# Transposes as two 64-row halves beside half-array matmuls in a PixArt block

## The chip, the core and the metric

The kernel runs on one core of a Trainium2 chip. The metric is the device time of one execution in microseconds (us); three runs of the kernel before have a median of 804.1 us. TensorE (PE) multiplies matrices into PSUM, VectorE (DVE) and ScalarE (ACT) work on PSUM and SBUF, GpSimd (POOL) on SBUF alone, and SyncE (SP) issues nearly all DMAs.

## The reference

A diffusion-transformer block for a batch of 16 sequences of 256 tokens with 256 features, all in float32: self-attention with 16 heads of 16, cross-attention to 256 context tokens, and an MLP of width 1024.

```python
x_norm = modulate(_ln(x), shift_a, scale_a)
q, k, v = split(x_norm @ W_qkv + b_qkv)              # 16 heads of 16
attn = softmax(q @ k.T * scale) @ v
x = x + gate_a[:, None] * (attn @ W_proj + b_proj)
q_c = _ln(x) @ W_qc + b_qc
k_c, v_c = split(_ln(context) @ W_kvc + b_kvc)
x = x + (softmax(q_c @ k_c.T * scale) @ v_c) @ W_cproj + b_cproj
x_norm2 = modulate(_ln(x), shift_m, scale_m)
x = x + gate_m[:, None] * (gelu(x_norm2 @ W_mlp1 + b_mlp1) @ W_mlp2 + b_mlp2)
```

## The kernel before, in words

The two attentions of a sequence are two *units*, a self unit (`s`) and a cross unit (`c`); 32 units run in a fixed order that soon alternates between the kinds. The MLP follows the last unit. A unit's stages are spread over several turns of the loop, so that each turn of `beat(n, k)`, k = 0 to 7, holds work of five or six units. All engines run in the order in which the program is written.

Float32 precision comes from pairs: a matrix is cut into a high part in the format fp32r (`xTh`, `h_q`) and the rest (`xTl`, `l_q`), and three products are added. A *lane* (`lane`) is a projection, Q, K, V or the output projection P, over one half of the contraction, 64 rows: 12 matmuls that use the upper or the lower half of the PE array. `lanes(x, y)` runs half 0 of one projection beside half 1 of another, matmul by matmul; both halves of a projection add into one PSUM tile, in two different beats. Names of lanes in the profile: `ps_q`, `ps_k`, `ps_v_s`, `ps_P_s` of self units, `ps_qc`, `ps_kc`, `ps_v_c`, `ps_P_c` of cross units.

Every beat begins with a *visit* (`visit`): four matmuls `s` of the next unit's scores, by which VectorE finds the maxima (`mx`, `s_tile`), and four matmuls `st` of this unit's transposed scores (`t_part`), which ScalarE exponentiates into `pt` (`exp`, gathered by `exps()`). `s` and `st` have two PSUM banks each and a single buffer; only in beat 6 of some units (`light`) half of `s` goes to another bank. Beats 0 and 4 hold the products with V (`av_part`, tile `o`, 16 matmul calls that the profile shows as 32), and beats 1, 3, 5 and 7 hold lanes.

Transposes with the full array come in between, through two shared PSUM buffers (tag `tr`, also used for `o`):

- `m_part` transposes the maxima (`psm`), ScalarE negates them, and SP sends them by DMA into row 63 of the queries: second half of unit n in beat 0, first half of unit n+1 in beat 4;
- `p1.turn(hf)` transposes the attention output (`psA`, four 128x128 pieces) in beats 2 and 6; VectorE divides by the sums (`norm`, tiles `rc` and `A`);
- `transposed(...)` makes the pair `xTh`, `xTl` of a normalized input (`psT_s`, `psT_c`, `psT_q`) or of `A` (`psT_as`, `psT_ac`), in beats 2, 4 and 6. `high` is ScalarE's. `low` is VectorE's for self units; elsewhere (`low_pool`) ScalarE makes a float32 copy `y` and GpSimd subtracts.

In PSUM, the tiles of lanes take turns in two buffers with the tag `gen`. The last three units (`whole`) project with the full array (`psP_c`), since the lanes run out.

Of the kernel before, what the change touches and what calls it, by code (L numbers as in the profile page):

```python
# [21 lines left out]
def pixart_block(  # L22
# [63 lines left out]
    vts = [const.tile([P, NT, NH, 32], F32, name=f"v{i}") for i in range(3)]  # L86
    wself = const.tile([P, 16, H], F32R, name="wself")
# [218 lines left out]

    def transposed(src, name, scale=None, pool=False):

        o = Box()

        def turn():
            o.ps = ps_gen(f"psT_{name}", SHORT)
            for f in range(KC):
                for t in range(NT):
                    PE.transpose(o.ps[:, f * N + t * P:f * N + (t + 1) * P],
                                 src()[:, t, f * P:(f + 1) * P], ident)
# [33 lines left out]
        o.turn, o.high, o.low = turn, high, low_pool if pool else low  # L350
        return o

# [17 lines left out]
    def lane(o, half):  # L370


        rows = slice(half * 64, half * 64 + 64)
        for low in (False, True):
            for f in range(2):
                for k in range(KC):
                    for a, b in (((1, 0),) if low else ((0, 0), (0, 1))):
                        xT, W = o.src.xT, o.W
                        x_, w_ = xT[a][rows, k], W[b][rows, k]
                        if o.tok:  # L380
                            x_ = x_[:, f * P:(f + 1) * P]
                        else:
                            w_ = w_[:, f * P:(f + 1) * P]
                        PE.matmul(o.ps[:, f * N:(f + 1) * N], *((x_, w_) if o.tok else (w_, x_)),
                                  start=o.fresh, stop=(half == 1 and low and k == KC - 1),
                                  skip_group_check=True)
                        o.fresh = False
                        yield

    def lanes(x, y):  # L390


        if x:
            x.ps, x.fresh = ps_gen(f"ps_{x.name}", LONG), True
        return zip_longest(*(lane(o, half) for half, o in enumerate((x, y)) if o))

    def run(steps, n=12):
        for _ in islice(steps, n):
            pass
# [92 lines left out]
    def build_pre(u):  # L492

        b = u.b
        u.mx = None
# [20 lines left out]
    def build_post(u):  # L516
# [17 lines left out]

        def turn(hf):
            o.ps = ps_gen(f"psA{hf}_{name}", SHORT)
            for t in range(NT):
                for r in range(2):
                    PE.transpose(o.ps[:, (2 * t + r) * P:(2 * t + r + 1) * P],
                                 u.oT[hf][:, r, t * P:(t + 1) * P], ident)  # L540
# [45 lines left out]
        u.post = o  # L586
# [8 lines left out]
    def s_tile(u, g, par, t, bank=None, home=sp):  # L595
# [14 lines left out]
        if u.mx is None:  # L610
            u.mx = work.tile([P, 2, 2, 4, NT], F32, tag="mx", name=f"mx_{u.n}", bufs=3)
        mx = u.mx.rearrange("p f r a t -> p r f a t")
        a = slice(2 * (g % 2), 2 * (g % 2) + 2)
        if alone or apart:
            src = home[bank] if apart else sp[:, bank]
            DVE.tensor_reduce(mx[:, par, g // 2, a, t], src.rearrange("p (j n) -> p j n", j=2),
                              AX.X, ALU.max)
        elif bank == 1:
            DVE.tensor_reduce(mx[:, :, g // 2, a, t], home.rearrange("p r (j n) -> p r j n", j=2),
                              AX.X, ALU.max)  # L620
        yield

    def m_part(u, hf):

        pst = ps_gen(f"psm_{u.n}_{hf}", SHORT)
        PE.transpose(pst[:16, :P], u.mx[:, hf].rearrange("p r a t -> p (r a t)"), ident)
        m = work.tile([16, P], F32R, tag="m", name=f"m_{u.n}_{hf}", bufs=1)
        ACT.mul(m, pst[:16, :P], -1.0)
        for par in range(2):
            SP.dma_start(u.q[par * 64 + 63:par * 64 + 64, 4 * hf:4 * hf + 4, :].bitcast(F32),  # L630
                         m[par * 8:(par + 1) * 8].bitcast(F32))
# [321 lines left out]

    def beat(n, k):
        if n < 0:
            visit(n, k, (st, sp)[k % 2])
            return
# [4 lines left out]
        whole = n > nu - 4  # L962
# [4 lines left out]
        q3T = q3  # L967
# [21 lines left out]
        visit(n, k, home)  # L989
        if k == 0:  # L990
            if cur:
                m_part(cur, 1)
            exps()
# [14 lines left out]
        elif k == 1:  # L1008
            exps()
            run(lanes(q2 and q2.Q, p2))  # L1010
# [3 lines left out]
        elif k == 2:  # L1014
            exps()
            if prev:
                p1.turn(1)
            if q3T:
                q3T.T[0].turn()
                q3T.T[0].high()  # L1020
            if prev:
                p1.norm(1)
            if p2 and p2.hurry:
                p2.add()
        elif k == 3:
            exps()
            if q3T and q3T.kind == "s":
                q3T.T[0].low()
            run(lanes(q2 and q2.V, q2 and q2.Q))
            if q3T and q3T.kind == "c":  # L1030
                q3T.T[0].low()
        elif k == 4:
            if nxt:
                m_part(nxt, 0)
            exps()
# [3 lines left out]
            if prev:  # L1039
                p1.aT.turn()  # L1040
                p1.aT.high()
# [11 lines left out]
        elif k == 5:  # L1053
            exps()
            run(lanes(q3 and q3.K, q2 and q2.V))
            if prev:
                p1.aT.low()
# [11 lines left out]
        elif k == 6:  # L1069
            exps()  # L1070
            if cur:
                cur.post.begin()
                cur.post.turn(0)
            if lx:
                lx.T[1].turn()
                lx.T[1].high()
# [3 lines left out]
            if prev and whole:  # L1080
                p1.proj(0)
                p1.proj(1)
        elif k == 7:
            exps()
            run(lanes(None if whole else p1, q3 and q3.K))
            if prev and whole:
# [5 lines left out]
            if lx:  # L1092
                lx.T[1].low()
# [97 lines left out]
```

## Time and profile before

| what | value |
|---|---|
| median of 3 runs | 804.1 us (802.99 to 809.25) |
| the profiled execution, first to last instruction | 801.2 us |
| busy time of PE, DVE, ACT, POOL | 780.7, 596.9, 583.5, 465.1 us |
| granted clock of TensorE, mean | 0.997 |
| GpSimd, subtraction of a low part, 128x512 | 1280 ns |
| ScalarE, high part, 128x512 | 588 ns |

The profiled execution is a run of its own; its span is 2.9 us under the median of the three, and no other time of it is given. Busy times overlap, and a busy PE need not be at its peak. In a profile row, "x4" is the count of instructions; `xTl_as<-y_as,xTh_as` reads output and inputs; what stands behind "idle" or in brackets names who ended the idle time ahead. A line number is that of a helper (L51) through which the kernel issues everything, so rows are told apart by the names of the tiles.

### The profile page before, as it was taken

To read this page: it belongs to the slowest core of one execution; us is meant where nothing else is said; L and a number is where in the kernel's file an instruction comes from. 1 tells how busy PE (TensorE), PEld (TensorE's weight loads), DVE (VectorE), ACT (ScalarE), POOL (GpSimd) and SP (SyncE) were. 2 spreads that over 40 slices of the span, in tenths; PEclk is the share of its full clock that TensorE was granted. 3 is DMA by queue.
4 is the path that set the end of the run, shared out by engine and by line. 5 is a ranking of instruction groups with operands and counts; after the bars stand their busy time and mean duration, and the time that the engine had idled before them with its cause. 6 is when DMAs were issued, how large, how long until landed. Compare 5 with 4: busy or idle time off the path is not lost.

```text
span 801.2 us, 23698 instructions
## 1 busy us (share of the span) xinstructions
PE 780.7 (97%) x9447; PEld 658.7 (82%) x9447; DVE 596.9 (74%) x1063; ACT 583.5 (73%) x1024; POOL 465.1 (58%) x405
## 2 busy tenths in 40 slices
PE   9999999999999999999999999999899999999997
PEld 8677777878878878877887787777669999999997
DVE  5887878788888878878888887876764656656662
ACT  4278888878888887878888788887656666666663
POOL 6745647565463756646475677563536656666653
PEclk9999999999999999999999999999999999999999
DMA  7554444434343453535445454534311322321211
GB/s 212 142 157 121 119 124 114 125 103 141 107 135 108 134 138 100 144 102 142 108 126 149 128 147 118 153 102 121 96 43 42 92 60 60 81 58 62 80 44 50
DMA packets 89938, 87.88 MB, mean 110 GB/s; under 512 B 9506, under 2 KB 85572, under 8 KB 89828
## 3 DMA queue, kind: packets, MB, share of 16 engines
q1 hardware_dynamic: 89364, 85.58, 38.4%
q8 instruction: 75, 1.23, 0.6%
q0 software_dynamic: 192, 0.52, 0.2%
q10 hardware_dynamic: 272, 0.26, 0.1%
q14 instruction: 35, 0.29, 0.1%
HBM read 26.97 MB, written 8.46 MB: 44 GB/s over the span
## 4 chain that ended last, share of the span: by engine, by line
PE 78%; DVE 11%; ACT 3%; DMA 3%; POOL 2%; issue 2%; ACTq 0%; SPq 0%; POOLq 0%; DVEq 0%
PE s L51 17%; PE o L51 14%; PE ph L51 11%; PE st L51 11%; DVE mx L51 8%; PE ps_qc L51 4%; PE ps_q L51 3%; PE ps_kc L51 3%; ACT pt L51 2%; PE ps_P_s L51 2%; PE ps_v_s L51 2%; PE ps_k L51 2%; PE psm L51 2%; PE ps_P_c L51 2%; PE ps_v_c L51 1%
## 5 line engine op out<-in xcount | busy, mean ns | idle before, releaser
L51 DVE TENSOR_REDUCE mx<-s 128x4 f32<-128x1024 f32 (+1 forms) x267 | 309.3, 1163 | 93.9 <-PE s L51 91.0
L51 ACT ACTIVATE pt<-st 128x1024 f32<-128x1024 f32 x252 | 256.7, 1019 | 39.9 <-PE st L51 34.3
L51 PE MATMUL s<-big 63*128 63x256 f32 (+1 forms) x1024 | 122.0, 309 | 6.6 <-DVE mx L51 3.7
L51 PE MATMUL o<-pt,v 128*32 128x256 f32 x2048 | 125.0, 385 | 0.0
L51 POOL TENSOR_TENSOR hl<-hf,hh 128x512 fp32r<-128x512 f32 x64 | 88.9, 1398 | 54.8 <-ACT hh L51 53.8
L51 PEld LDWEIGHTS s<-big 63*128 63x128 f32 (+1 forms) x1024 | 80.8, 185 | 41.9 <-DVE mx L51 18.8
L51 PE MATMUL st<-big 64*128 64x256 f32 (+1 forms) x1024 | 108.7, 283 | 4.9 <-ACT pt L51 4.0
L51 PEld LDWEIGHTS o<-pt,v 128*32 128x32 f32 x2048 | 60.3, 110 | 41.2 <-issue 0.8
L51 PEld LDWEIGHTS st<-big 64*128 64x128 f32 (+1 forms) x1024 | 82.2, 186 | 9.5 <-ACT pt L51 7.2
L51 ACT ACTIVATE hf<-ph,bT 128x256 f32<-128x256 f32 x120 | 50.3, 473 | 28.1 <-PE ph L51 28.1
L51 ACT COPY oT<-o 128x512 f32<-128x512 f32 x63 | 37.0, 587 | 43.8 <-PE o L51 43.8
L51 ACT ACTIVATE hh<-ph,bT 128x256 fp32r<-128x256 f32 x120 | 50.4, 472 | 23.7 <-PE st L51 11.9
L51 POOL TENSOR_TENSOR xTl_c<-y_c,xTh_c 128x512 fp32r<-128x512 f32 x16 | 20.5, 1281 | 61.7 <-PE s L51 52.5
L51 POOL TENSOR_TENSOR xTl_as<-y_as,xTh_as 128x512 fp32r<-128x512 f32 x16 | 20.5, 1280 | 55.5 <-ACT y_as L51 55.5
L51 PE MATMUL ph<-wqch,wself 128*128 128x256 f32 x256 | 51.8, 285 | 0.0
L51 PE MATMUL ph<-wkch,wself 128*128 128x256 f32 x256 | 51.8, 286 | 0.0
L51 POOL TENSOR_TENSOR xTl_ac<-y_ac,xTh_ac 128x512 fp32r<-128x512 f32 x16 | 20.5, 1284 | 52.4 <-ACT y_ac L51 48.4
L51 PE MATMUL s<-big,hh 128*128 128x256 f32 x256 | 47.4, 282 | 0.0
L51 PE MATMUL st<-big,hh 128*128 128x256 f32 x256 | 47.2, 281 | 0.0
L51 DVE TENSOR_SCALAR xn_m<-x,mv_m,rs_m 128x256 f32<-128x256 f32 x32 | 38.3, 1238 | 11.4 <-POOL rs_m L51 11.4
L51 PEld LDWEIGHTS ph<-wqch,wself 128*128 128x128 f32 x256 | 42.0, 191 | 0.4 <-issue 0.4
L51 PEld LDWEIGHTS ph<-wkch,wself 128*128 128x128 f32 x256 | 41.9, 191 | 0.4
(223 smaller groups left out, 2378.1 us busy)
## 6 DMA issues: line engine op xcount, KB each, us to landing
big<-h_kc SPq DMA_DIRECT2D x64, 128.0 KB
big<-h_qc SPq DMA_DIRECT2D x64, 128.0 KB
big<-h_k SPq DMA_DIRECT2D x62, 128.0 KB
big<-h_q SPq DMA_DIRECT2D x62, 128.0 KB
big<-l_k SPq DMA_DIRECT2D x32, 128.0 KB
big<-l_q SPq DMA_DIRECT2D x32, 128.0 KB
c<-in_ctx_dram SPq DMA_DIRECT2D x16, 256.0 KB
g<-gd SPq DMA_DIRECT2D x16, 256.0 KB
```

Source lines behind the costliest of these rows:

```text
L51: i = f(*a, **k)
```

## The change

Every transpose inside the units becomes two halves of 64 rows each, which are written to 64 columns each of the same PSUM bank, and each half runs beside lane matmuls in the other half of the array. Between the two halves stands an instruction of TensorE that waits for the last matmul of the half before (`after`); lanes get such a wait ahead of half 1 too. `transposed` gets an `evac` (ScalarE, float32 copy) and a `cut` (GpSimd: cast to the high part, then subtraction). The maxima lie in fixed tiles of 160 columns, so that their transpose has 128 columns of weights; GpSimd zeroes these tiles at the start.

```diff
+    def after(name):
+        gate = PE.nop()
+        tc.add_manual_dep(gate.ins, name, mybir.DependencyInfo(
+            mybir.DependencyClass.Sync, mybir.DependencyReason.DATA), reason="one bank, two halves of the array")
+
+    def half_turns(pieces, o):
+        done = []
+        def half(h):
+            rows = slice(64 * h, 64 * h + 64)
+            for i, p in enumerate(pieces):
+                if i == 0 and done:
+                    after(done[0])
+                ins = PE.transpose(o.ps[:, i * P + 64 * h:i * P + 64 * h + 64], p[rows], ident[rows, rows])
+                if i == len(pieces) - 1:
+                    done.append(ins.ins.name)
+                yield
+        return half(0), half(1)
...
+        def evac():
+            y = o.y = work.tile([P, KC, N], F32, tag="y", name=f"y_{name}", bufs=2)
+            if scale is None:
+                ACT.copy(y.rearrange("p k n -> p (k n)"), o.ps)
+            else:
+                for f in range(KC):
+                    ACT.activation(y[:, f], o.ps[:, f * N:(f + 1) * N], AF.Identity, scale=scale[f])
+
+        def cut():
...
+            POOL.tensor_copy(hi, o.y)
+            POOL.tensor_tensor(lo, o.y, hi, ALU.subtract)
...
+        if half:
+            after(o.seen)
...
+    def take(it, n):
+        for _ in range(n):
+            next(it, None)
+            yield
+
+    def beside(a, b):
+        for _ in zip_longest(chain(*a), chain(*b)):
             pass
...
         visit(n, k, home)
+        exps()
         if k == 0:
-            if cur:
-                m_part(cur, 1)
-            exps()
...
         elif k == 1:
-            exps()
-            run(lanes(q2 and q2.Q, p2))
+            m = m_halves(cur, 1) if cur else none
+            x, y = lane0(q2 and q2.Q), lane1(p2)
+            beside([m[0], x], [take(y, 4), m[1], y])
+            if cur:
+                m_send(cur, 1)
...
         elif k == 2:
-            exps()
-            if prev:
-                p1.turn(1)
-            if q3T:
-                q3T.T[0].turn()
-                q3T.T[0].high()
-            if prev:
-                p1.norm(1)
+            T = q3.T[0].halves() if q3 else none
+            A = p1.halves(1) if prev else none
+            x, y = lane0(q2 and q2.V), lane1(q2 and q2.Q)
+            beside([T[0], A[0], take(x, 2)], [take(y, 10)])
+            rest_x, rest_y = [x], [T[1], A[1], y]
...
         elif k == 3:
-            exps()
-            if q3T and q3T.kind == "s":
-                q3T.T[0].low()
-            run(lanes(q2 and q2.V, q2 and q2.Q))
-            if q3T and q3T.kind == "c":
-                q3T.T[0].low()
+            beside(rest_x, rest_y)
+            if q3:
+                q3.T[0].evac()
+                q3.T[0].cut()
+            if prev:
+                p1.norm(1)
         elif k == 4:
-            if nxt:
-                m_part(nxt, 0)
-            exps()
             if cur:
                 av_part(cur, 0)
                 av_part(cur, 1)
-            if prev:
-                p1.aT.turn()
-                p1.aT.high()
...
         elif k == 5:
-            exps()
-            run(lanes(q3 and q3.K, q2 and q2.V))
+            m = m_halves(nxt, 0) if nxt else none
+            aT = p1.aT.halves() if prev else none
+            x, y = lane0(q3 and q3.K), lane1(q2 and q2.V)
+            beside([m[0], take(x, 7), aT[0], x], [take(y, 2), aT[1], m[1], y])
+            if nxt:
+                m_send(nxt, 0)
             if prev:
-                p1.aT.low()
+                p1.aT.evac()
+                p1.aT.cut()
...
         elif k == 6:
-            exps()
             if cur:
                 cur.post.begin()
-                cur.post.turn(0)
-            if lx:
-                lx.T[1].turn()
-                lx.T[1].high()
+            T = lx.T[1].halves() if lx else none
+            A = cur.post.halves(0) if cur else none
+            y = lane1(q3 and q3.K)
+            beside([T[0], A[0]], [take(y, 8 if lx else 4)])
+            rest_y = [T[1], A[1], y]
...
         elif k == 7:
-            exps()
-            run(lanes(None if whole else p1, q3 and q3.K))
-            if prev and whole:
+            beside([lane0(None if apart else p1)], rest_y)
+            if lx:
+                lx.T[1].evac()
+                lx.T[1].cut()
+            if prev and apart:
```

`lane0` opens a projection's PSUM tile and yields half 0, `lane1` yields half 1, `m_halves` yields the two halves of the maxima's transpose, and `m_send` is the second part of the old `m_part`.

More of the change, by code (lines that the diff above doesn't have):

```diff
@@ L1 @@
 from collections import defaultdict
-from itertools import islice, zip_longest
+from itertools import chain, zip_longest
 from contextlib import ExitStack
@@ L86, in pixart_block @@
     vts = [const.tile([P, NT, NH, 32], F32, name=f"v{i}") for i in range(3)]
+    mxs = [const.tile([P, 160], F32, name=f"mx{i}") for i in range(3)]
+    for t_ in mxs:
+        POOL.memset(t_, 0.0)
     wself = const.tile([P, 16, H], F32R, name="wself")
@@ L350, in transposed @@
         o.turn, o.high, o.low = turn, high, low_pool if pool else low
+        o.halves, o.evac, o.cut = halves, evac, cut
         return o
@@ L533, in gate, with pieces, halves @@
             POOL.tensor_tensor(o.xg, X[b], bc_t(G[b][:, 1]), ALU.add)
+        def pieces(hf):
+            o.ps = ps_gen(f"psA{hf}_{name}", SHORT)
+            return [u.oT[hf][:, r, t * P:(t + 1) * P] for t in range(NT) for r in range(2)]
         def turn(hf):
[L536 to L540, printed above, removed]
+            whole(pieces(hf), o)
+        def halves(hf):
+            return half_turns(pieces(hf), o)
         def norm(hf):
```

71 lines of the change are left out of this document (42 added, 29 removed).

## The prediction

> **What bounds the kernel now.** I read the page's head and its chain of work first, then the busy time by stretches for two neighbouring units, then the timeline of one unit, engine by engine.
>
> ```profile
> span 801.2 us, 23698 instructions
> PE 780.7 (97%) x9447; PEld 658.7 (82%) x9447; DVE 596.9 (74%) x1063; ACT 583.5 (73%) x1024; POOL 465.1 (58%) x405
> PE 78%; DVE 11%; ACT 3%; DMA 3%; POOL 2%; issue 2%; ACTq 0%; SPq 0%; POOLq 0%; DVEq 0%
> ```
>
> ```profile
> 402.65:419.86 17.21, 17.00 (x246) 13.59 (x244) 15.58 (x30) 14.10 (x23) 11.90 (x11) 1.00 0.42 115
> 419.86:437.25 17.39, 17.29 (x251) 14.01 (x249) 13.43 (x22) 14.58 (x24) 7.56 (x8) 1.00 0.47 128
> ```
>
> Columns of the second fence: stretch, its length, then busy time of PE, PEld, DVE, ACT, POOL, granted clock, DMA share, GB/s. TensorE is busy all the time at full clock, and the chain is 78% TensorE. The first unit works on a cross-attention unit (call it C), the second on a self-attention unit (S); a pair takes 34.60 us. But VectorE has 15.58 of 17.21 us in C: there is little room below TensorE's time.
>
> One unit C on TensorE. Each `s` row that opens a visit starts a beat; the beats k=0 to 7 start at 402.65 (the stretch's start), 405.30, 407.29, 409.04, 411.03, 414.27, 416.26 and 417.45.
>
> ```profile
> 403.23 0.28 PE L51 MATMUL psm<-ident,mx 128*16 128x128 f32 x1
> 403.44 1.93 PE L51 MATMUL o<-pt,v 128*32 128x256 f32 x32
> 405.30 0.50 PE L51 MATMUL s<-big 63*128 63x256 f32 x4
> ...
> 407.29 0.42 PE L51 MATMUL s<-big 63*128 63x256 f32 x4
> 407.53 0.42 PE L51 MATMUL st<-big 64*128 64x256 f32 x4
> 407.88 0.66 PE L51 MATMUL psA_s<-ident,oT 128*128 128x128 f32 x4
> 408.38 0.60 PE L51 MATMUL psT_s<-ident,xn_s 128*128 128x128 f32 x4
> 409.04 0.50 PE L51 MATMUL s<-big 63*128 63x256 f32 x4
> ...
> 409.61 0.28 PE L51 MATMUL ps_v_c<-wvch,xTh_c 64*128 64x256 f32 x1
> ...
> 411.03 0.42 PE L51 MATMUL s<-big 63*128 63x256 f32 x4
> 411.62 0.28 PE L51 MATMUL psm<-ident,mx 128*16 128x128 f32 x1
> 411.82 1.93 PE L51 MATMUL o<-pt,v 128*32 128x256 f32 x32
> 413.69 0.66 PE L51 MATMUL psT_as<-ident,A_s 128*128 128x128 f32 x4
> 414.27 0.50 PE L51 MATMUL s<-big 63*128 63x256 f32 x4
> 416.26 0.43 PE L51 MATMUL s<-big 63*128 63x256 f32 x4
> 417.45 0.51 PE L51 MATMUL s<-big 63*128 63x256 f32 x4
> 418.11 0.50 PE L51 MATMUL st<-big 64*128 64x256 f32 x4
> ```
>
> Three prices come out of it. A slot (one half-array matmul in each half): 12 pairs from 409.61 to 411.03, so 0.118 us. A visit (`s` and `st`, four slots) is 0.47, and 0.57 right after full-array work (409.04 to 409.61), so 0.10 for the change of mode. A full transpose is 0.11: four of them take 0.60 (`psT_s`), one takes 0.28 (`psm`), and (0.60 - 0.28)/3 = 0.107.
>
> There is a second limit, the loop of the scores: `s` must wait until VectorE has reduced the last ones.
>
> ```profile
> 407.76 1.23 DVE L51 TENSOR_REDUCE mx<-s 128x4 f32<-128x1024 f32 x1
> 408.90 0.25 DVE L51 RECIPROCAL rc_s<-psA_s 128x16 f32<-128x16 f32 x1
> 409.18 0.42 DVE L51 TENSOR_TENSOR A_s<-psA_s,rc_s 128x256 f32<-128x256 f32 x1
> ```
>
> In k=2 `s` starts at 407.29, the reduce at 407.76, it ends at 408.99, and the next `s` is at 409.04: no ordinary beat can be shorter than 1.75 us, whatever TensorE saves in it.
>
> **The change, beat by beat.** TensorE first.
> - k=0 and k=4 lose `psm` (403.23 to 403.44 and 411.62 to 411.82: 0.2 each), k=4 also the four transposes of `A` (413.69 to 414.27: 0.58). Both become 2.44 to 2.46 (before 2.65 and 3.24).
> - k=1 has 13 slots instead of 12: 1.99 + 0.12 = 2.11. k=5 has 17: 1.99 + 5 x 0.118 = 2.58.
> - k=2 loses 8 full transposes (407.88 to 409.04, 1.16 with the drain) and gets 10 slots, 1.18; k=3 goes from 12 slots to 10 and has no mode to change. Both would be 0.47 + 1.18 = 1.65, so the score loop sets them: 1.75. k=2 gains nothing, k=3 0.24.
> - k=6 of S: 8 slots, 1.41, loop again, 1.75 as now. k=6 of C uses a second bank for `s` and goes below the loop; 4 slots, 0.94. k=7: 12 slots, 0.47 + 1.42 = 1.88, before about 2.0 in S.
>
> In C, k=7 now lasts 2.41 because `st` at 418.11 waits for ScalarE:
>
> ```profile
> 416.50 0.61 ACT L51 COPY v<-ps_v_c 128x512 f32<-128x512 f32 x1
> 417.03 1.02 ACT L51 ACTIVATE pt<-st 128x1024 f32<-128x1024 f32 x1
> ```
>
> That exponential stays behind `y` and `v`, which come later after a longer k=5: I place it 0.75 to 1.77 after k=6 starts, so `st` of k=7 at 1.84, and 0.24 + 1.42 of `st` pairs and slots behind it: k=6 and k=7 together 3.5, now 3.60.
>
> Then what VectorE, ScalarE and the waits give back. `norm(1)` (0.68, from 408.90 to 409.58) moves from k=2 to the end of k=3, ahead of the reduce of k=4. In S it pushes reduce, `l_q` and statistics so that the reduce of k=5 ends late: I estimate 0.03. In C, statistics and `rs_c` ahead of the reduce of k=2 make that beat an estimated 1.83. The scaled `y_s` of a self unit is two ScalarE passes like this one, behind the exponential of k=3:
>
> ```profile
> L51 ACT ACTIVATE xTh_s<-psT_s,sc 128x256 fp32r<-128x256 f32 x32 | 13.4, 472 | 6.6 <-PE psT_s L51 5.1 <-DVE sc L51 1.5
> ```
>
> They end about 2.6 after k=3 starts (the exponential from 0.75, its successor 0.9 later, then 2 x 0.47). `o` of k=4 takes the bank that they read and could start at 1.75 + 0.58 = 2.33, so it starts 0.25 late. VectorE is freed of `xTl_s`, two passes a pair. The self wait: for all but one of the ten or so waits in a unit, the last matmul of the first half lies at least six slots, 0.7 us, back, against 0.28 that a matmul takes: no stall. The transposes of `A` in k=5 alone have two slots between (0.24): one stall of 0.05 to 0.15, I take 0.1. A wait itself lies between 0 and the 0.10 of a mode change; I take 0, since five of them stand in beats that the score loop sets.
>
> C: 2.44 + 2.11 + 1.83 + 1.75 + 2.69 + 2.68 + 3.5 = 17.0. S: 2.44 + 2.11 + 1.75 + 1.75 + 2.44 + 2.68 + 1.75 + 1.88 + 0.03 = 16.8. The pair is 33.8 against 34.6: 0.8 gained. Bounds: with no give-back (0.08 + 0.25 + 0.03 and two stalls of 0.1) 1.4; with each wait outside the loop's beats (six a unit) at 0.05, 0.2.
>
> GpSimd makes both parts now. Its prices:
>
> ```profile
> L51 POOL TENSOR_TENSOR xTl_as<-y_as,xTh_as 128x512 fp32r<-128x512 f32 x16 | 20.5, 1280 | 55.5 <-ACT y_as L51 55.5
> L51 POOL CAST wkch<-wkc_f 128x512 fp32r<-128x512 f32 x1 | 0.6, 610 | 5.7 <-DMA wkc_f<-in_L_xcond_W_kvc_dram 5.7
> L51 POOL TENSOR_SCALAR xn_c<-c,mv_c,rs_c 128x256 f32<-128x256 f32 x32 | 38.9, 1224 | 1.7
> L51 POOL TENSOR_TENSOR rs_q<-rs_q,mhalf 128x2 f32<-128x2 f32 x16 | 11.4, 712 | 11.8 <-DVE rs_q L51 11.8
> L51 POOL TENSOR_TENSOR hl<-hf,hh 128x512 fp32r<-128x512 f32 x64 | 88.9, 1398 | 54.8 <-ACT hh L51 53.8
> ```
>
> Five casts (3.05) and one subtraction more (1.28): 19.5 + 4.3 = 23.8 of 33.8 us, not a bound by sum. The cover that matters is its queue in C. From `y_ac` in k=5 of S it does cast, subtraction, `rs_s`, `xn_s`, cast, subtraction, three adds of `x1` and its gate (1.28 each), `rs_c`, `xn_c`, and then the cast that k=5 of C needs in slot 2: 3 x 0.61 + 5 x 1.28 + 2 x 0.71 + 4 x 1.22 = 14.5, 14.9 with gaps. By my beats 14.9 is there. It costs nothing, with no reserve.
>
> The maxima go to the queue one beat later, and this moves SP's order:
>
> ```profile
> 411.75 2.48 SPq L51 DMA_DIRECT2D big<-h_qc  x4
> 414.33 1.42 SPq L51 DMA_DIRECT2D big<-m  x2
> 415.85 1.28 SPq L51 DMA_DIRECT2D big<-l_qc  x2
> ...
> 451.14 3.76 DMA big<-l_qc
> ```
>
> `l_qc` no longer stands behind `m`: it leaves up to 1.4 us earlier, and `m`, behind it, I estimate to land over half a us before its `st` (a stall of that length, were the estimate wrong). `l_qc` is on the chain now and then. From the first row below (k=0 of a C unit) to 437.25 (the end of the second stretch, the same place) are ten pairs, 34.86 each, so 0.26 more than the clean pair; I credit 0.15 of it, bounds 0 and 0.26.
>
> ```profile
> 88.68 0.40 PE L51 MATMUL s<-big 63*128 63x256 f32 x3
> ```
>
> 28 of 32 units run like this, 14 pairs: 14 x (0.8 + 0.15) = 13.3. The last three units have no lanes beside the transposes and wait for one cast more each: + 1.8. Three memsets of 128x160 on GpSimd ahead of everything (some 0.25 each, from the 0.204 of 128x128 below) lie under the first weight loads and TensorE's warm-up; uncovered they would cost 0.7.
>
> ```profile
> masks.py:197 POOL MEMSET ident<- 128x128 f32 x1 | 0.2, 204 | 0.3 <-POOLq L1179 0.3
> ```
>
> Sum: 801.2 - 13.3 + 1.8 = 789.7 of the profiled span; the three runs' median lies 2.9 above the span, so 792.6, say 793.
>
> **Rivals.**
> - *The halves don't overlap.* No row shows an F32 transpose in one half beside a matmul in the other. If its stream of 64 columns (half of a full one, 0.055) is added to the slot, the beats without reserve (k=1, 5, 7: 20 halves in S, 16 in C) lose 0.99 a unit, k=2 and k=3 0.58 after their 0.1 to 0.18 of reserve, and k=6 0.1: 28 x 1.67 = + 47, so 840. At the full 0.11 it would be near 900. It decides from 0.02 us a half on. For it: the kernel never mixes kinds in the halves. Against it: the two F32R lanes overlap fully, 0.118 for two. The Trainium skill, page TensorEngine Tiling (Array Packing), Key Properties, says that different tiles can run loads and matmuls in parallel; by that this price is zero, and the trace agrees for two like lanes (0.118) and shows nothing of mixed ones.
> - *GpSimd's queue decides.* Its chain has no reserve. If its instructions stretch by 5%, 0.75 a pair is gone and the result is 804, no change; at the 9% of the `hl` row (1398 against 1280 for the same shape) it is 811. For it: VectorE is busier per us than before. The Trainium skill, page GPSIMD Engine Reference, Key points, says that GpSimd shares its SBUF interfaces with VectorE, and contends with instructions of two SBUF inputs; the row below agrees, a tiny VectorE instruction with 169 ns at best and 1206 at worst. Against it: VectorE's reduces, most of its time, read PSUM, and the subtractions beside them took 1280.
>
> ```profile
> L51 DVE TENSOR_SCALAR rs_c<-mv_c x16: 169/452/1206, 58.1 to 512.8; 128x2 f32<-128x2 f32 x16
> ```
>
> - *The self wait restarts TensorE.* If each wait empties the queue like a change of mode (0.10), 6 exposed waits a unit cost 28 x 0.6 = 17, so 810; from 0.08 us a wait on nothing is left.
>
> **How the numbers follow.** About 1% (8 us) can be told from no change here. Forecast 0.56, halves that don't overlap 0.17, GpSimd's queue 0.17, the waits 0.10. The forecast's own range is 783 (no give-back, all of the DMA stall gone) to 803. Within it, about three in four lie beyond 1%: faster 0.43. Same: the quarter of the forecast, most of GpSimd's case, a third of the waits: 0.29. Slower: 0.28. The range has to reach the first rival's lower price: 783 to 840.
>
> **What would show it.** Right: `psm` and `A` transposes gone from k=0 and k=4, those beats 2.45; k=5 near 2.6 to 2.7; k=2, k=3 at 1.75 with `s` waiting for `mx`; a pair of 33.5 to 34.0; GpSimd near 24 of a pair; slots of 0.118 with a transpose in one half. Wrong: slots over 0.14 beside a transpose; `ps_k` or `ps_kc` waiting for the `xTh` cast by over 0.3 us a pair; gaps of 0.1 at every self wait; or beats of 1.65 where I set 1.75.

## The result, and the profile after

The changed kernel takes 799.75 us (median of 20 runs, 797.42 to 803.25), the kernel before 803.97 (20 runs beside it, 801.08 to 809.25). The ratio is 0.9944, 95% interval 0.9927 to 0.9960: 4.2 us faster, 0.6%, where the forecast was 793 and 11 us. The direction was right, the size was off by more than half. The profiled span went from 801.2 to 797.9, where 789.7 was forecast: a miss of 8.2 us, against 7 in the median, because a time lies 1.7 to 1.9 us above its span in every run of the changed kernel, and the 2.9 of before held 1 us of a profiled execution below its median.

The page's head and chain, as shown of before:

```profile
span 797.9 us, 25010 instructions
...
PE 771.4 (97%) x10066; PEld 668.6 (84%) x10066; DVE 589.5 (74%) x1037; ACT 557.1 (70%) x961; POOL 529.4 (66%) x497
...
PE 60%; DVE 15%; POOL 9%; ACT 8%; issue 4%; DMA 2%; SPq 1%; POOLq 0%; ACTq 0%
```

TensorE's share of the last chain fell from 78% to 60%; VectorE, GpSimd and ScalarE took it up. The same two units as before (C, then S), by stretches:

```profile
402.01:419.05 17.04, 16.77 (x265) 13.95 (x263) 14.90 (x28) 13.77 (x22) 15.33 (x16) 1.00 0.44 120
419.05:436.08 17.03, 16.89 (x271) 14.31 (x271) 13.46 (x22) 13.26 (x21) 8.48 (x9) 1.00 0.48 132
```

The pair is 34.07 us (before 34.60, predicted 33.8); GpSimd's 15.33 + 8.48 = 23.81 is what was forecast (23.8). Unit C on TensorE in the changed kernel; beats start at 402.01, 404.53, 406.62, 408.37, 410.19, 412.89, 415.34 and 416.65:

```profile
402.01 0.49 PE L51 MATMUL s<-big 63*128 63x256 f32 x4
...
402.66 1.93 PE L51 MATMUL o<-pt,v 128*32 128x256 f32 x32
404.53 0.50 PE L51 MATMUL s<-big 63*128 63x256 f32 x4
...
406.62 0.43 PE L51 MATMUL s<-big 63*128 63x256 f32 x4
...
407.10 0.22 PE L51 MATMUL psT_s<-ident,xn_s 64*128 64x64 f32 x1
407.13 0.28 PE L51 MATMUL ps_qc<-xTh_q,wqch 64*128 64x256 f32 x1
407.16 0.28 PE L51 MATMUL psT_s<-ident,xn_s 64*128 64x64 f32 x2
407.25 0.27 PE L51 MATMUL ps_qc<-xTh_q,wqcl 64*128 64x256 f32 x1
407.28 0.22 PE L51 MATMUL psT_s<-ident,xn_s 64*128 64x64 f32 x1
407.35 0.22 PE L51 MATMUL psA_s<-ident,oT 64*128 64x64 f32 x1
407.37 0.28 PE L51 MATMUL ps_qc<-xTh_q,wqch 64*128 64x256 f32 x1
...
408.37 0.50 PE L51 MATMUL s<-big 63*128 63x256 f32 x4
...
410.19 0.50 PE L51 MATMUL s<-big 63*128 63x256 f32 x4
...
412.89 0.51 PE L51 MATMUL s<-big 63*128 63x256 f32 x4
...
415.34 0.28 PE L51 MATMUL s<-big 63*128 63x256 f32 x1
...
416.65 0.51 PE L51 MATMUL s<-big 63*128 63x256 f32 x4
```

All beats, C from these starts and S from the unit behind it (no transfer is late in either):

| | k0 | k1 | k2 | k3 | k4 | k5 | k6 | k7 | unit |
|---|---|---|---|---|---|---|---|---|---|
| C predicted | 2.44 | 2.11 | 1.83 | 1.75 | 2.69 | 2.68 | 3.5 with k7 | | 17.0 |
| C measured | 2.52 | 2.09 | 1.75 | 1.82 | 2.70 | 2.45 | 1.31 | 2.40 | 17.04 |
| S measured | 2.50 | 2.10 | 1.75 | 1.82 | 2.53 | 2.45 | 1.96 | 1.93 | 17.03 |
| S predicted | 2.44 | 2.11 | 1.75 | 1.75 | 2.44 | 2.68 | 1.75 | 1.88 | 16.8 |

Two places divide the whole run: the first `s` of unit 4 and that of unit 28 (numbered from 0), here before, then after.

```profile
106.06 0.41 PE L51 MATMUL s<-big 63*128 63x256 f32 x4
526.35 0.41 PE L51 MATMUL s<-big 63*128 63x256 f32 x4
```

```profile
107.93 0.50 PE L51 MATMUL s<-big 63*128 63x256 f32 x4
523.70 0.57 PE L51 MATMUL s<-big 63*128 63x256 f32 x4
```

| part of the span | forecast | measured |
|---|---|---|
| start to unit 4 | 3 units of -0.47: -1.4 | 107.93 - 106.06: +1.9 |
| 12 clean pairs | 12 x -0.80: -9.6 | 12 x -0.53: -6.4 |
| lateness of transfers and all other waits in these 24 units | 12 x -0.15: -1.8 | +1.9 (what is left of 415.77 - 420.29 = -4.5) |
| unit 28 to the end | -0.5 + 1.8: +1.3 | -0.7; +1.2 without the slower clock in the trace of before |
| span | -11.5 | -3.3; -1.5 without it |

So 3.2 us went in the clean pair, 3.7 in the waits of the third row and 3.3 in the head. The 2 us that the tail seems to give back are not the change's: in the profiled execution of before, TensorE's granted clock was 0.50 for 3.4 us, and `o` of the last unit took 3.12 us where it takes 1.93 after. The stretch of before (columns as above) and the two `o`, before and after:

```profile
584.89:588.30 3.41, 3.41 (x32) 1.59 (x20) 1.12 (x3) 1.32 (x2) 1.58 (x2) 0.50 0.25 86
584.30 3.12 PE L51 MATMUL o<-pt,v 128*32 128x256 f32 x32
582.60 1.93 PE L51 MATMUL o<-pt,v 128*32 128x256 f32 x32 [0.18 <-DVE A_c L51]
```

From the `s` ahead of it to the next `s` are 6.88 us before (581.50 to 588.38) and 5.04 after (580.01 to 585.05), so 1.84 is the clock's; with it the miss of 8.2 becomes the 10.2 of the three. No such stretch lies between the starts of unit 0 and unit 28 in either trace.

The transfer: k=4 of the self units is 2.53 when nothing is late, but 3.15, 2.83, 3.31, 2.72, 3.16, 2.87 and 3.62 in seven of the twelve self units from unit 4 on, 4.0 us over 2.53 in all (the nine units named in the expectation of experiment 1 are a miscount). This is one execution: in that of experiment 5, whose program is the same, the sum is 1.8. The transfer of the worst of them (unit 24) in the chain of waits (start, length, what):

```profile
459.28 3.55 DMA big<-m
```

And SP's queue in k=0 and k=1 of a self unit, before (unit 16) and after (unit 24); columns are start, duration, what is issued and how often:

```profile
316.52 2.93 SPq L51 DMA_DIRECT2D big<-h_k  x3
319.56 1.42 SPq L51 DMA_DIRECT2D big<-m  x2
321.08 1.28 SPq L51 DMA_DIRECT2D big<-l_k  x2
322.42 0.58 SPq L51 DMA_DIRECT2D x<-in_x_dram  x1
```

```profile
454.07 3.07 SPq L51 DMA_DIRECT2D big<-h_k  x4
457.24 1.21 SPq L51 DMA_DIRECT2D big<-l_k  x2
458.54 1.43 SPq L51 DMA_DIRECT2D big<-m  x2
460.01 0.43 SPq L51 DMA_DIRECT2D w<-in_L_xcond_W_mlp_dram  x1
```

The second half of the maxima went from ahead of `l_k` to behind it, and, in every self unit from 4 to 22, behind the load of `x` (256 KB) too, which before stood behind `l_k`. In unit 24, where no `x` stands in front of it, it landed 3.55 us after its issue; its reader is only three beats further on. In experiment 5 the same beat of unit 24 takes 2.53, so the order alone doesn't make a landing late.

### The profile page after: what moved, and what is told of

Same layout as the page of the kernel before. It is cut to its first block, busy times and chain, and to the rows that moved or that the text cites. A ratio compares the mean times of both kernels' runs of the same rounds, so it can differ in the third digit from the quotient of the medians.

```text
span 797.9 us, 25010 instructions
## 1 busy us (share of the span) xinstructions
PE 771.4 (97%) x10066; PEld 668.6 (84%) x10066; DVE 589.5 (74%) x1037; ACT 557.1 (70%) x961; POOL 529.4 (66%) x497
## 3 DMA queue, kind: packets, MB, share of 16 engines
q8 instruction: 80, 1.31, 0.7%
## 4 chain that ended last, share of the span: by engine, by line
PE 60%; DVE 15%; POOL 9%; ACT 8%; issue 4%; DMA 2%; SPq 1%; POOLq 0%; ACTq 0%
PE o L51 14%; PE s L51 10%; PE st L51 7%; DVE mx L51 6%; DVE xn_m L51 4%; PE ps_qc L51 3%; PE ps_q L51 3%; POOL hl L51 3%; PE ps_v_c L51 3%; PE ps_P_s L51 3%; PE ph L51 3%; PE ps_k L51 2%; PE ps_v_s L51 2%; PE ps_kc L51 2%; PE ps_P_c L51 2%
## 5 line engine op out<-in xcount | busy, mean ns | idle before, releaser
L51 ACT ACTIVATE pt<-st 128x1024 f32<-128x1024 f32 x252 | 259.5, 1030 | 79.8 <-PE st L51 68.2
L51 PE MATMUL s<-big 63*128 63x256 f32 (+1 forms) x1024 | 132.7, 315 | 4.1 <-DVE mx L51 1.8
L51 PEld LDWEIGHTS s<-big 63*128 63x128 f32 (+1 forms) x1024 | 86.5, 185 | 44.6 <-DVE mx L51 10.7
L51 PE MATMUL st<-big 64*128 64x256 f32 (+1 forms) x1024 | 116.2, 285 | 6.7 <-ACT pt L51 4.1
L51 PEld LDWEIGHTS st<-big 64*128 64x128 f32 (+1 forms) x1024 | 89.0, 186 | 12.2 <-ACT pt L51 6.7
L51 POOL CAST xTh_c<-y_c 128x512 fp32r<-128x512 f32 x16 | 10.0, 626 | 56.5 <-ACT y_c L51 51.0
L51 PE MATMUL ps_k<-xTh_s,wself 64*128 64x256 f32 (+1 forms) x232 | 41.5, 293 | 0.0
L51 PE MATMUL ps_v_s<-wself,xTh_s 64*128 64x256 f32 x224 | 41.5, 295 | 0.0
```

The lines of the kernel that those rows point to most:

```text
L51: i = f(*a, **k)
```

## The experiments

My theory after the comparison: the slots and the self waits cost what was forecast or less; the loss is (Q) the place of the maxima in SP's one queue, (B) beats that stay bound by something other than TensorE, so that removed work there buys nothing, and (H) a head that no term of the sum covered. The rivals: the waits (W), GpSimd's queue (R2). All edits are against the changed kernel unless said otherwise. The kernel before, run beside each of them, has medians from 802.68 to 804.26 us, so a difference of about 1 us between two experiments is not told; where it matters, the ratio to the kernel before is given (0.9944 for the changed kernel, 0.9927 to 0.9960).

**1. `l_k` behind the maxima.**

```
 k == 0:      q2.K.low()
-             q2.K.send_low()
 k == 1:      m_send(cur, 1)
+             q2.K.send_low()
```

> The changed kernel with one edit: the transfers of l_k (two of 128 KB a unit) are issued behind the maxima in k=1, not in k=0. Theory Q (the place of the maxima in SP's queue): in 9 of the 12 self units from the 4th to the 27th k=4 is 0.2 to 1.1 us over its shortest 2.53, 4.0 us together, because the second half of the maxima stands behind l_k and the load of x and lands after its reader; with l_k behind them that sum falls below 1 us, and the time from 799.8 to about 796 (795 to 797.5). Rival G (GpSimd's queue holds these beats back): k=4 stays as it is, 799 to 800.5. Rival X (only the load of x, which still stands ahead of the maxima, matters): k=4 improves by under a quarter, 799.

Measured: 799.60 us (12 runs, 798.30 to 802.66). k=4 of all twelve self units is 2.53 or 2.54: the 4.0 us over 2.53 became 0.05. The beat that was worst, k=4 of unit 24, from its `s` to the next:

```profile
465.36 0.50 PE L51 MATMUL s<-big 63*128 63x256 f32 x4
...
467.89 0.50 PE L51 MATMUL s<-big 63*128 63x256 f32 x4
```

Theory Q holds for the beat. The time did not follow (795 to 797.5 was expected, and rival X's 799 is nearer; it is the beat that speaks against X): k=7 grew by 0.07 to 0.09 in every unit (2.40 to 2.46, 1.93 to 2.02), 1.9 over the 24 units, which then took 414.1 instead of 415.8. What lengthens k=7 was not found. The profiled execution was 3.1 us over the median: TensorE's granted clock was 0.72 and 0.76 in it from 20 to 40 us, before any edit matters.

**2. The load of `x` behind the maxima.**

```
 k == 0:
-            if ls and n > 0:
-                load(ls)
 k == 1:     m_send(cur, 1)
+            if ls and n > 0:
+                load(ls)
```

> The changed kernel with one edit: the load of x (256 KB, every second unit) is issued behind the maxima in k=1, not ahead of them in k=0. Theory Q: x is one third of what stands between h_k and the maxima (l_k 256 KB, x 256 KB, and their issue 1.2 + 0.6 us), so a part of the 4.0 us goes, 1.5 to 3: 797 to 798.5. Rival X (x alone decides): 795.5 to 796.5, and the first kernel of this call 799. Rival G: 799 to 800.5.

Measured: 797.48 us (6 runs, 797.04 to 799.46), in the better half of what Q expected; the ratio is 0.9930 (0.9908 to 0.9953), which overlaps with the changed kernel's. k=4 of the self units is over 2.53 by 0.5 in all. So in these two executions taking either of the two transfers away from in front of the maxima was enough, which speaks against `x` alone (the first kernel) and against `x` as a third of it (this one). It isn't proof: unit 24, which loads no `x` and which this edit leaves as it was, went from 3.62 to 2.53 too. In the profiled execution (the slowest of the six) other transfers were late in its place: k=0 and k=1 of the cross units are 3.9 us over their shortest, 0.6 in the changed kernel, and the 24 units take 415.6 against 415.8. One of them is the load of `c`, in front of statistics that stand ahead of a score reduce:

```profile
434.74 4.55 DMA c<-in_ctx_dram
```

**3. The load of `c` moved away as well.** Experiment 2 and, in addition:

```
 k == 2:
+            v = unit(n + 5)
+            if v and v.kind == "c":
+                load(v)
 k == 5:     (the same three lines left out)
```

> The kernel with the load of x behind the maxima, and the load of c (256 KB, every second unit) issued in k=2 in place of k=5, where SP stands still between the maxima and h_q. In the profile of x behind the maxima, k=4 of the self units was down to 2.53, but three cross units lost 1.05, 1.2 and 1.1 us, two of them since c landed 4.6 us after its issue and the statistics in front of the score reduce waited for it. Theory Q (one SP queue, whose order decides what is late): these two go and nothing new appears, 797.5 - 2 = 795.5 (794.5 to 797). Rival B (the transfers are short of bandwidth as a whole, so another one becomes late): 797 to 799, with the same sum of lateness at another beat.

Measured: 798.74 us (6 runs, 796.17 to 800.67). The lateness of `c` in the cross units is gone, but the maxima were late in k=4 of unit 4 (3.52) and in k=0 of unit 23 (3.85). Rival B: the queue hands the lateness on. No gain over experiment 2 can be told from this.

**4. The maxima whole again, in k=0 and k=4.**

```
 k == 0:     +   m_part(cur, 1)        k == 1:  m halves, m_send left out
 k == 4:     +   m_part(nxt, 0)        k == 5:  m halves, m_send left out
```

> The changed kernel with the maxima transposed whole in k=0 and k=4 and sent there, as before the change; all other transposes stay in halves. k=0 and k=4 are then 2.65 again (measured now 2.51 and 2.53), k=1 and k=5 lose one slot of 0.118 each and k=5 of the self unit one self wait. Theory Q: the late landings of k=4 (4.0 us) and the 1.1 us in the first unit go, + 28 x 2 x 0.13 = + 7.3 for k=0 and k=4, - 28 x 2 x 0.11 = - 6.2: together 795.5 to 797. If the maxima's place has nothing to do with those 5 us: 800 to 801.

Measured: 807.58 us (8 runs, 805.99 to 810.90), a miss by 11. k=4 of the self units is 2.79 or 2.80 in all twelve, so the maxima's lateness is gone here too, as Q has it. What I missed is the price of the whole transpose in this kernel:

```profile
233.33 0.50 PE L51 MATMUL s<-big 63*128 63x256 f32 x4
...
233.99 0.33 PE L51 MATMUL psm<-ident,mx 128*128 128x128 f32 x1
234.25 1.93 PE L51 MATMUL o<-pt,v 128*32 128x256 f32 x32
```

From `s` to `o` are 0.92 us, 0.27 more than without `psm` (402.01 to 402.66). The maxima now lie in a 160-column tile, and the whole transpose loads 128 columns where the one before the change loaded 16. That is 56 x 0.27 = 15, against 28 x 0.11 = 3 saved in k=1 (k=5 stayed at 2.46) and the 4 of the maxima.

**5. Every self wait twice.**

```
+        for _ in range(2):
             gate = PE.nop()
             tc.add_manual_dep(gate.ins, name, ...)
```

> The changed kernel with every self wait of TensorE issued twice, some ten more a unit. Forecast's term (a wait whose matmul has ended costs nothing): 799 to 801. Rival W (a wait restarts TensorE, 0.05 to 0.1 us each, six a unit outside the beats that the score loop sets): + 8 to + 17, so 808 to 817; then taking the waits away would be worth as much.

Measured: 800.04 us (12 runs, 797.26 to 803.48) against 799.75. The edit does nothing: built, it gives the changed kernel's program again, every engine with the same instructions and the same semaphore waits in the same order (25010 instructions in both profiles). So this run is a second measurement of the changed kernel, 0.3 apart, and says nothing of the price of a wait. What speaks against W are the beats: k=1 holds two such waits and takes 2.10, where the forecast had 2.11 with the waits at nothing, and k=5 to k=7 come out at their sums, though there transposes that are cheaper than a slot could hide a part. A test that takes the waits away or adds real ones is open.

**6. The parts as before the change.**

```
-  q3.T[0].evac(); q3.T[0].cut()      (likewise p1.aT and lx.T[1])
+  q3.T[0].high(); q3.T[0].low()
```

> The changed kernel with the parts made as before the change: ScalarE writes the high part from PSUM, VectorE the low part of self units, GpSimd the other low parts; GpSimd's five casts and one subtraction a pair (4.3 us) are gone. Rival R2 (GpSimd's queue holds TensorE back): faster, 795 to 798. My reading of the profile (no wait on a cast among the waits of TensorE, but y_s late for o in k=4): GpSimd's share costs nothing, ScalarE and VectorE get 0.87 a self unit back, 799 to 803.

Measured: 821.24 us (5 runs, 819.86 to 824.27), 21 us slower than the changed kernel; the ratio to the kernel before is 1.0232 (1.0208 to 1.0256). R2's forecast (faster) fails: GpSimd works less and the pair takes longer, 36.12 us with 19.49 of GpSimd (columns as in the stretches above):

```profile
345.08:363.65 18.57, 16.89 (x263) 14.17 (x262) 16.09 (x31) 14.65 (x25) 12.38 (x12) 1.00 0.42 117
363.65:381.20 17.55, 17.34 (x272) 14.64 (x271) 13.23 (x21) 14.10 (x24) 7.11 (x7) 1.00 0.48 127
```

I expected 799 to 803. Half of the pair's 2.05 lies in k=4 of C (3.69 against 2.69), where the bracket names what ended TensorE's idle time; k=4 of S and k=0 of C have 0.40 each:

```profile
353.65 0.50 PE L51 MATMUL s<-big 63*128 63x256 f32 x4
...
355.48 1.93 PE L51 MATMUL o<-pt,v 128*32 128x256 f32 x32 [1.06 <-DVE xTl_s L51]
```

`o` of k=4 waits for the bank of `psT_s`. With halves spread over k=2 and k=3 the transposes end late; if then both parts are read out of PSUM, ScalarE's and after it VectorE's pass keep the bank until 1.1 us after TensorE wants it. One quick copy to SBUF, from which GpSimd makes both parts, lets go of the bank earlier (`o` of this beat starts 0.83 after its `s` in the changed kernel, 1.83 here). Since the edit loads ScalarE and VectorE and holds the bank at once, it can't tell by itself what GpSimd's queue costs.

**7. The transposes of k=2 whole again.**

```
 k == 2:  p1.turn(1); q3.T[0].turn()          (no lanes)
 k == 3:  beside([lane0(q2.V)], [lane1(q2.Q)])   evac, cut, norm(1) as now
```

> The changed kernel with the transposes of k=2 (xn and the second half of oT) whole again, ahead of nothing but k=2's visit, and the lanes of V and Q back in k=3 with 12 slots; the rest of the change stays. By the score loop: k=2 stays at 1.74, k=3 goes from 1.83 to 1.99, + 28 x 0.16 = + 4.5, so 803 to 805.5. If halves are worth what the eight transposes take (1.16 us less two slots): k=2 would be 2.2 or k=3 shorter, + 10 and more. If they are worth nothing here: 799 to 801.

Measured: 800.91 us (11 runs, 798.42 to 804.15), 1.2 more than the changed kernel, scatter included. Clean units take 16.95 (C) and 17.11 (S), the pair 34.06: the same as with halves. k=3 is 2.00 instead of 1.82 as expected, but k=4 is 2.44 instead of 2.70 in C and 2.53 in S. In whole form the transposes end early and `o` finds its bank free, and `s` of k=4 takes 0.42 (at 445.43), where that of k=3 takes 0.50 (at 443.43).

So this part of the change, eight of a unit's 18 (C) or 22 (S) transposes, is worth nothing that can be told: 1.16 us of transposes were removed from a beat that the score loop sets.

**8. 11 and 9 slots instead of 10 and 10.**

```
-  beside([T[0], A[0], take(x, 2)], [take(y, 10)])
+  beside([T[0], A[0], take(x, 3)], [take(y, 11)])
```

> The changed kernel with 11 slots in k=2 and 9 in k=3 in place of 10 and 10. k=3 takes 1.83 and not the 1.75 of the loop that I had put down, and its s starts 0.04 after the reduce that it waited for, on an idle array, and takes 0.50 instead of 0.41. Theory L (the loop is 1.75 only where s follows on work, 1.83 where TensorE stood still): k=2 becomes 1.77, s of k=3 follows on, k=3 is 1.75: - 28 x 0.05 = - 1.4, so 798 to 799. Rival (the array's state doesn't matter): k=2 1.77 and k=3 1.80 to 1.83, 799.5 to 801.

Measured: 800.30 us (12 runs, 799.66 to 802.80), k=2 1.74 and k=3 1.83. No change; theory L in this form is not borne out. One half of the array works up to the `s` of k=3 now, for the third `ps_qc` of the first row starts 0.07 ahead of it, and `s` takes 0.50 all the same:

```profile
409.27 0.51 PE L51 MATMUL ps_qc<-xTl_q,wqch 64*128 64x256 f32 x3
409.57 0.50 PE L51 MATMUL s<-big 63*128 63x256 f32 x4
```

Two things still set this `s` apart from that of k=4 in experiment 7: the other half of the array has nothing left to do, and `s` starts right behind the reduce that it waits for. Which of them makes it longer is open.

**9. Both halves of `xn`'s transposes in k=2.**

```
-  beside([T[0], A[0], take(x, 2)], [take(y, 10)])
-  rest_x, rest_y = [x], [T[1], A[1], y]
+  beside([T[0], A[0], take(x, 4)], [take(y, 6), T[1], take(y, 2)])
+  rest_x, rest_y = [x], [A[1], y]
+  q3.T[0].evac(); q3.T[0].cut()               (in k=3 left out)
```

> The changed kernel with both halves of the transposes of xn in k=2 (the second half beside the lane of Q, where the score loop leaves TensorE over half a us), and its copy and cut at the end of k=2 in place of k=3. Theory B (the bank: o of k=4 takes the bank that y_s and y_c are read from, so k=4 is 2.69 in a cross unit and 2.53 in a self unit, and 2.44 and 2.44 where the transposes were whole in k=2): k=4 becomes 2.44 in both, k=3 stays at 1.83, - 14 x 0.34 = - 4.8, so 795 (794 to 797). Rival E (ScalarE: the copy now stands ahead of the exponential of k=3, 0.94 in a cross unit, and what is gained in k=4 comes back in k=4 or k=5 as a wait for it): 798.5 to 801.

Measured: 799.44 us (12 runs, 797.04 to 801.61). k=4 of C goes from 2.69 to 2.53 and k=5 from 2.45 to 2.58; the pair is 33.96, 0.1 less. Half of theory B: the wait for the bank is gone, 0.16; the other 0.09 over 2.44, in both kinds, stays, so it is no bank. k=5 took most of it back. Rival E's wait isn't in the rows there (ScalarE's exponential of k=5 starts 0.85 after the beat in both kernels); what lengthens k=5 is open.

The edit has a price at the ends of the batch that I overlooked. GpSimd's cast and subtraction now stand ahead of the add that makes `x1` in its queue; in units 2 and 28, where the norm of `x1` is late, the statistics wait for that add and the reduce stands behind them. k=5 of these units is 3.00 and 3.53, and 3.25 and 3.52 in experiment 10, where unit 2 has these rows; it was 2.44 and 2.72 in the changed kernel, where that cast starts at 81.15, behind the add (79.28).

```profile
79.00 0.61 POOL L51 CAST xTh_c<-y_c 128x512 fp32r<-128x512 f32 x1 [4.48 <-ACT y_c L51]
82.30 1.29 POOL L51 TENSOR_TENSOR x<-xg,t_s 128x512 f32<-128x512 f32 x1
83.61 0.75 DVE L51 BATCH_NORM_STATS2 st_q<-x 128x6 f32<-128x256 f32 x2 [0.88 <-POOL x L51]
```

**10. Experiments 2 and 9 together.**

> The kernel with both halves of xn's transposes in k=2, and with the load of x behind the maxima as well. If the two gains lie in different beats they add: - 4.8 - 2.3, so 792.7 (791 to 795). If the shorter units only make another transfer late (one queue, 34.06 a pair now and 33.7 then): 795 to 797, with the lateness in k=0 or k=1 of the cross units.

Measured: 796.50 us, six runs between 796.20 and 796.61, ratio 0.9917 (0.9898 to 0.9936) to the kernel before: the lowest median here and clearly below the kernel before; its interval just overlaps with the changed kernel's. No self unit has k=4 over 2.54. It is 3.25 below the changed kernel and not the 7 expected, since experiment 9 gave 0.1 a pair and not 0.34: 14 x 0.1 and the 2.3 of experiment 2 are 3.7. The spread is 0.4 us in six runs, where the changed kernel had 5.8 in twenty, but experiment 11, with the same edits and more, has 3.3 in six. Part of the scatter goes with the clock: the five shortest times of the changed kernel have a mean granted clock of 0.998 to 1.000, the four longest 0.995 to 0.997. That transfers which land just in time or just late make the rest was not tested.

**11. The head.** Experiment 10 and, in addition:

```
 k == 0:  +  if cur and n < 2: m_part(cur, 1)     (k == 1: halves and m_send for n > 1 only)
-  (0, 2): 'd3',                                  three filler matmuls
```

> The same two edits, and in the first two units the second half of the maxima is transposed whole and sent in k=0, as before the change, and the three filler matmuls behind k=2 of the first unit are left out. The first four units cost the changed kernel 1.9 us against the kernel before (1.1 a wait for the maxima, 0.7 the fillers behind a k=2 that is full now): 1.5 to 2 less than the kernel with the two edits alone. If the head's loss is only handed on to the next units, as part of it was before (the lag was 2.1 at the second unit and 1.5 at the third): under 0.7.

Measured: 796.57 us (6 runs, 796.03 to 799.34): nothing. In the profiles unit 1 begins 1.7 earlier (53.15 against 54.89) and unit 4 2.1 earlier (106.93 against 109.05). The two are hard to compare, since the granted clock of experiment 10's is 0.91 from 88 to 106 us; why nothing is left of this at the end is open. What neither edit touches is a wait that the changed kernel has more of than the one before (waits of TensorE from 50 to 145 us, before, then after; columns are the total, how often, the longest):

```profile
PE psT_q L51 <- POOL xn_q L51: 0.7, 2, 0.3
```

```profile
PE psT_q L51 <- POOL xn_q L51: 1.7, 2, 0.8
```

In the first and last units of the batch the norm of `x1` starts only in k=4 and its transposes are due in k=6. My reading is that this chain does not get shorter while k=4 and k=5 did, by 0.70 less 0.46, so that TensorE waits longer for the same thing.

**12. That norm one beat earlier.** Experiment 10 and, in addition:

```
 k == 3:  p1.norm(1)
+         if late:
+             for f in lx.ln[1].steps: f()
 k == 4:  (the same left out)
```

> The kernel with both halves of xn's transposes in k=2 and the load of x behind the maxima, and one edit more: in the units where the norm of x1 is late (units 2, 4, 27, 28 and the like, the first and the last of the batch), its statistics, rs_q and xn_q are issued at the end of k=3 and not of k=4. Theory H (in these units the gain of the change went into a chain of fixed length: rs_q on VectorE, 0.71 and 2.44 of GpSimd, then psT_q in k=6; TensorE waited 0.3 for xn_q before the change and 0.8 after it, in each of five units): k=6 falls from 2.51 to 1.95 and k=7 from 2.17 to 1.93, - 0.8 in each, - 3 to - 4 together: 796.5 - 3.5 = 793 (792.5 to 794). Rival D (the statistics now stand ahead of the score reduce of k=4 and lengthen it by their 1.2): k=4 grows by 0.5 or more in these units, 795 to 797.

Measured: 801.73 us (12 runs, 799.56 to 805.18). In unit 4 k=6 and k=7 fell to 1.96 and 1.93 as theory H has it. But rival D came, and larger than I put it: statistics that wait for `x1` block VectorE's queue ahead of the reduce, which opens the next `s`; k=4 of unit 2 is 5.76 and that of unit 28 6.13. Its mean granted clock is lower too, 0.988 to 0.995 in the twelve runs (0.995 to 1.000 in the changed kernel's), so not all of the 5 us over experiment 10 need be these waits. VectorE there, then TensorE:

```profile
83.66 0.75 DVE L51 BATCH_NORM_STATS2 st_q<-x 128x6 f32<-128x256 f32 x2 [2.84 <-POOL x L51]
...
84.74 1.22 DVE L51 TENSOR_REDUCE mx<-s 128x4 f32<-128x1024 f32 x1
```

```profile
86.01 0.79 PE L51 MATMUL s<-big 63*128 63x256 f32 x4 [3.15 <-DVE mx L51]
```

## Why the prediction was wrong in size, and where it was right

**The step that failed most: the maxima in SP's queue.** I wrote that `m`, behind `l_qc`, lands over half a us before its `st`, with "a stall of that length, were the estimate wrong". For `l_qc` the step was right: k=0 was over its shortest by 2.6 us in all in these 24 units before, and no wait for `l_qc` is left among TensorE's waits there. But I looked at one of the two moves only. The other half of the maxima went behind `l_k`, and I did not see the load of `x`, a transfer of 256 KB that this puts ahead of them as well. The maxima's lateness is 4.0 us in the profiled run; with the 2.6 of k=0 gone (0.5 of it is named as waits for `l_qc`) and 1.0 more of waits for `xn_q` in units 4 and 27, a term of -1.8 became +1.9. In experiments 1, 2 and 4 something is taken from in front of the maxima, and the lateness of k=4 goes each time, to 0.5 us or less. How much time it costs is less sure: the sum is 1.8 in another execution of the same program (experiment 5), the median of experiment 1 did not move, and that of experiment 2 fell by 2.3.

**The clean pair: terms mis-sized by 0.27.** Three beats with `o` were put at 2.44; k=0 is 2.52 and 2.50 and k=4 of S 2.53, 0.23 a pair. C's 2.69 came out by luck: of the 0.25 that I put down for the bank, experiment 9 shows 0.16, and the other 0.09 is what k=4 of S has too. k=3 was put at the loop's 1.75, and is 1.82. The 1.75 came from a k=2 whose `s` follows on work (`s` 0.42 in k=2 of before); in k=3, where `s` starts right behind the reduce that it waits for, it takes 0.50, and its own reduce starts 0.08 later. I had both lengths in the quoted rows and generalized the shorter. Work in one half of the array up to that `s` didn't shorten it (experiment 8). Against it, k=2 of C is 1.75, not 1.83. With 0.02 less in k=1 that is 0.23 + 0.14 - 0.08 - 0.02 = 0.27, the 34.07 against 33.8.

**The head, in no term.** I counted 14 pairs of the batch's 16 as clean. The units up to 3 lost 3.3 against that: 1.1 for the maxima, late behind three weight loads, 0.7 for filler matmuls in a k=2 that is full now, and the wait for `xn_q`. Experiment 11 takes the first two away and experiment 12 moves the third, and neither is faster than experiment 10. That the chain behind `x1` sets these units is my reading, not shown.

**The tail: right in size by luck.** Without the slower clock in the trace of before it is +1.2, and +1.3 was forecast. But the cast in front of `psP`, put at 1.8, is not what it went to. The waits of TensorE from 500 us to 640 us have

```profile
PE psT_q L51 <- POOL xn_q L51: 2.2, 3, 0.8
PE psP_c L51 <- POOL xTh_ac L51: 0.2, 1, 0.2
PE psP_c L51 <- POOL xTl_ac L51: 0.2, 1, 0.2
```

where `xn_q` had 0.7 before, and unit 28 alone takes 1.0 longer than before, where 0.5 less was forecast.

**Right:** the beats k=5 to k=7 together (S predicted 6.34, measured 6.34; C 6.18 and 6.16), though with another split: half transposes are cheaper than a slot, and the next `s` starts in one half while the other still works (415.34: `s` one by one). k=1, and k=2 of S. GpSimd's 23.8. The waits at nothing, as far as the beats show it (k=1 at its sum). *Halves that don't overlap* was wrong altogether, by the rows of k=2 above: the four half transposes of `psT_s` and the first of `psA_s` start within 0.25 us (407.10 to 407.35), so 0.06 each, while `ps_qc` in the other half keeps its 0.12 (407.13, 407.25, 407.37). The Trainium skill's sentence on tiles that run in parallel (TensorEngine Tiling (Array Packing), Key Properties) holds here for unlike work too. *GpSimd's queue decides* was wrong for the clean units, where no cast and no subtraction is among TensorE's waits. At the ends of the batch it has a part: TensorE's waits for GpSimd's `xn_q` are 1.3 us in the whole run before and 3.8 after, and in experiment 9 the order of that queue costs 0.6 and 0.8 in two beats.

**Open:** what lengthens k=7 in experiment 1 and `s` behind its reduce, the 0.07 of k=0 over 2.44, why the time follows the repaired beats only in part, what a self wait costs, and which part of the head's 3.3 each of its three causes has, since they hide behind one another.

## What to carry to other kernels

When work moves from one beat to another, list what it issues and write down the queue's order before and after for every kind of unit, loads included; a small transfer can pay for all that it is put behind. Before counting removed work as gain, ask for each beat what ends it: a transpose taken out of a beat that another loop sets was worth nothing here, and it may come back where its result, or its PSUM bank, is due next. Units at the ends of a batch have their own chains and need a term of their own. Before a difference between two traces is read as work, look at the granted clock of that stretch, and before a run is read as a test, see that the edit has changed the built program.

## What the runs showed of the hardware that I had not expected

- F32 transposes of 64 rows by 64 columns in one half of the array follow each other in 0.06 us, beside matmuls of 256 columns in the other half that keep their 0.118.
- TensorE's granted clock was 0.50 for 3.4 us in one profiled execution and lengthened one beat by 1.84 us (6.88 against 5.04), over half of the difference between the two spans.
- A whole transpose between half-array matmuls and the 32-column `o` took 0.14 where it loads 16 columns (0.79 from `s` to `o` before the change, 0.65 without it) and 0.27 where it loads 128 (0.92).
- A tiny VectorE instruction (`rs_c`, 128x2) took 169 ns in the three places of before where no GpSimd instruction runs beside it, and 203 to 1206 ns in the other thirteen.
